# Masked queries shared between VectorE and ScalarE, and steps of short chains spread over their half-slots

## The chip, the cores and the metric

The kernel runs on one NeuronCore of a Trainium2 chip. A core has five engines that run side by side, each with a queue of its own, and wait for each other by semaphores: TensorE (PE in the profile; its weight loads are PEld), VectorE (DVE), ScalarE (ACT), GpSimd (POOL) and SyncE (SP, which here only issues DMAs). TensorE writes its results to PSUM, from which VectorE or ScalarE move them to SBUF. The metric is the device time of one execution in microseconds.

## What is computed

A decoder layer over 32 sequences of 128 tokens with 128 features, 16 heads of 8 features each: causal self-attention, cross-attention to a second input, and a mixture of 8 experts of which each token takes two. After each of the three comes a residual and a layer norm.

```python
def _attn(q_in, k_in, v_in, wq, bq, wk, bk, wv, bv, wo, bo, causal):
    Q = (q_in @ wq + bq).reshape(Bq, Sq, H, HD)
    Kp = (k_in @ wk + bk).reshape(Bq, Sk, H, HD)
    V = (v_in @ wv + bv).reshape(Bq, Sk, H, HD)
    scores = jnp.einsum('bqhd,bkhd->bhqk', Q, Kp) / jnp.sqrt(jnp.float32(HD))
    if causal:
        scores = jnp.where(mask, scores, -jnp.inf)
    a = jax.nn.softmax(scores, axis=-1)
    o = jnp.einsum('bhqk,bkhd->bqhd', a, V).reshape(Bq, Sq, Dm)
    return o @ wo + bo
...
x = _layernorm(x + _attn(x, x, x, ..., True), ln1_g, ln1_b)
x = _layernorm(x + _attn(x, encoder_output, encoder_output, ..., False), ln2_g, ln2_b)
x = _layernorm(x + _moe(x, router_w, router_b, e_w1, e_b1, e_w2, e_b2), ln3_g, ln3_b)
```

All arithmetic that matters here is in float32.

## The kernel before

**Stages.** First attention, then the experts. The attention works on groups of four sequences: eight groups of self-attention (named s0 to s7) and eight of cross-attention (c0 to c7). A unit is one sequence of one group, so there are 64 units, and units of s and c groups are interleaved in the list `order` (L1014). The experts' part runs 78 blocks of 128 rows, each with weights fetched from DRAM; its first blocks run beside the last steps of attention.

**Half-slots.** The attention is a software pipeline written out by hand. Each unit has two half-slots (`half_slot`, L1164). In half-slot h, TensorE first computes scores (`both_scores`, L437): for the unit t = h // 2 with queries as rows, eight heads at a time, into the PSUM buffer `sc` of which there is one, and for the unit t − 2 the same scores with keys as rows into `st`, of which there is one as well. VectorE takes the row maxima of `sc` (L487), which frees it; ScalarE takes the exponential of `st` (L495), which frees that. The maxima are split into three bfloat16 parts on GpSimd (`split`), turned round on TensorE and spread (`maxima`, L524, VectorE), and subtracted within the matmuls of `st`. In even half-slots TensorE also multiplies the probabilities of unit t − 3 with the values (`values`, 32 matmuls, evacuated by ScalarE at L541), in odd ones it turns the result round (`outputs`, two transposes, divided on VectorE at L552 and L553). Self-attention units have more matmuls for the causal mask (L442), and GpSimd clears the masked probabilities (L499).

**Masks of heads.** Heads lie four to a quarter of 32 partitions. A matmul that reads a quarter sees four heads at once, so the queries are stored four times, each time with all but every fourth head set to zero. `queries` (L400) projects two sequences at a time into a PSUM tile `pq` and writes the four masked copies into `qb` with four activations (L407) of 128 x 256, each as (pq + bias) times a mask column. A group has two such steps, so there are 32 of them and 128 activations. `qb` has four buffers; the experts' part uses the same ones later for `gt`.

**Steps beside the units.** Everything else of a group is cut into steps that are put into half-slots behind the work of the units: `turn_input` (transposes, evacuated by ScalarE), `keys`, `queries`, `values_of`, and after the group's units `turn_output` (two steps: transposes, evacuated by ScalarE at L564), `project` (seven steps: two projections with residual on VectorE at L573 and L576, then `normalize` at L331 with statistics on VectorE, the reciprocal root on GpSimd, and the scaling on ScalarE in two steps), then `hand_over` or `keep_x2` (four steps: two transposes with affine evacuation, two GpSimd steps). Cross-attention groups go on with `route`, `place`, `biases` and the scatter of their rows. `half_slot` calls the steps of its number from `table` in the order in which they were put there, and this is the order in the queues of all engines.

**The planner.** `chain(lo, hi, *parts)` (L1054) puts a list of steps, in order, into the half-slots lo to hi. Each step goes by `book` (L1043) to the half-slot in its window in which the busiest engine is least loaded; `busy` holds the loads, in microseconds estimated by hand, as a tuple of TensorE, VectorE, ScalarE and GpSimd. The costs of steps are given by `pe(us, act, dve)`, `dve` and `pool`. When a chain has more steps than half-slots are left, `book` gets an empty window and the steps at its front share the half-slot lo, until the remaining ones fit one to each.

For example the output chain of cross-attention group 0 has 13 steps for half-slots 45 to 54. Before, `turn_output` twice and both projections stand in 45, and the rest one to each half-slot from 46, with the last normalization step at 50 and `keep_x2` from 51. That of self-attention group 0 has five half-slots, 15 to 19, and its first nine steps (both `turn_output`, all seven of `project`) stand in 15.

**Fetches.** Groups 2 to 7 of self-attention are fetched by `fetch` (L118) on SyncE's queue, put at half-slot h0 − 15, where h0 is the first of the group's units. `xg` has three buffers, and one comes free when the group three before has added its residual in `project`. The same queue carries the packing of expert weights into DRAM, `pack` (two DMAs of 256 KB for each of the eight experts, at half-slots 4, 8, ... 32).

Of the kernel before, what the change touches and what calls it, by code (L numbers as in the profile page):

```python
# [8 lines left out]
F32 = mybir.dt.float32  # L9
# [4 lines left out]
AF = mybir.ActivationFunctionType  # L14
ALU = mybir.AluOpType
AX = mybir.AxisListType

P = 128
# [5 lines left out]
G = 4  # L24
# [38 lines left out]
def kernel(  # L63
# [34 lines left out]
    nc = tc.nc  # L98
# [6 lines left out]
    act = ctx.enter_context(tc.tile_pool(name="act", bufs=2))  # L105
# [74 lines left out]
    hmask = const.tile([P, 4], F32, name="hmask")  # L180
# [179 lines left out]
    def rowsof(g):  # L360
        return slice(32 * g, 32 * g + 32)
# [37 lines left out]

    def queries(gr):  # L400

        gr.qb = act.tile([P, G, 4, P], F32, tag="qb", name=f"qb_{gr.name}", bufs=4)
        for ab in PAIRS:
            pq = pair(f"pq_{gr.name}", ab)
            nc.tensor.matmul(pq, lhsT=gr.w.wq, rhs=gr.qT[:, ab], start=True, stop=True)
            for r in range(4):
                nc.scalar.activation(  # L407
                    gr.qb[:, ab, r, :], pq, AF.Identity,
                    bias=gr.w.bqm[:, r : r + 1], scale=hmask[:, r : r + 1],
                )  # L410
            yield

    turn = {"v": -1, "m": 0}
# [23 lines left out]
    def both_scores(new, old, half):  # L437


        def mask(g, i, j):  # L440
            k = slice(32 * j, P)
            nc.tensor.matmul(  # L442
                sc[:, i, :, k], lhsT=quarter[rowsof(g), j, :],
                rhs=bc(causal[rowsof(g), j, k], 1, 4), start=j == 0, stop=False,
            )

        def by_query(g, i, r):
            nc.tensor.matmul(  # L448
                sc[:, i, r, :], lhsT=new.group.qb[rowsof(g), new.b, r, :],
                rhs=new.group.k[rowsof(g), new.b, :],  # L450
                start=not new.masked, stop=not new.masked or r == 3,
            )

        def less_maxima(g, i, _):
            nc.tensor.matmul(
                st[:, i], lhsT=ones16[rowsof(g), :], rhs=old.mq[rowsof(g)], start=True, stop=False
            )

        def by_key(g, i, r):
            nc.tensor.matmul(  # L460
                st[:, i, r, :], lhsT=old.group.k[rowsof(g), old.b, :],
                rhs=old.group.qb[rowsof(g), old.b, r, :], start=False, stop=r == 3,
            )

        steps = []
        if new is not None:
            sc = ps_sc.tile([P, 2, 4, P], F32, tag="sc", name=f"sc_{new.name}_{half}")
            at_us = 0.0
            if new.masked:
                for j in range(RG):  # L470
                    steps.append((at_us, 1, mask, j))
                    at_us += 0.053 * (RG - j)
            for r in range(4):
                steps.append((at_us, 1, by_query, r))
                at_us += 0.222
        if old is not None:
            st = ps_st.tile([P, 2, 4, P], F32, tag="st", name=f"st_{old.name}_{half}")
            steps.append((0.0, 0, less_maxima, 0))
            steps += [(0.213 + 0.222 * r, 0, by_key, r) for r in range(4)]

        for _, query, do, n in sorted(steps, key=lambda step: step[:2]):
            for i in range(2):
                do(2 * (half if query else 1 - half) + i, i, n)
        if new is not None:
            if half == 0:
                new.m = small.tile([P, H], F32, tag="m", name=f"m_{new.name}")
            nc.vector.tensor_reduce(  # L487
                new.m[:, 8 * half : 8 * half + 8], sc.rearrange("p i r k -> p (i r) k"),
                AX.X, ALU.max,
            )  # L490
        if old is not None:
            if half == 0:
                old.pr = prob.tile([P, H, P], F32, tag="pr", name=f"pr_{old.name}")
            hs = slice(8 * (1 - half), 8 * (1 - half) + 8)
            nc.scalar.activation(  # L495
                old.pr[:, hs, :], st.rearrange("p i r k -> p (i r) k"), AF.Exp, scale=SCALE
            )
# [526 lines left out]
    def at(h, *call):  # L1024
        table.setdefault(h, []).append(call)
        return h + 1
# [3 lines left out]
    for t, u in enumerate(units):  # L1030
        for h, cost in (
# [8 lines left out]
            old = busy.get(2 * t + h, (0.0,) * 4)  # L1040
# [13 lines left out]
    def chain(lo, hi, *parts):  # L1054


        todo = []
        for made, *costs in parts:
            if len(costs) == 1:
                todo.append((costs[0], (made,)))  # L1060
                continue
            steps = []

            def step(made=made, steps=steps):
                if not steps:
                    steps.append(made())
                next(steps[0], None)

            todo += [(cost, (step,)) for cost in costs]
        ends = []  # L1070
        for n, (cost, call) in enumerate(todo):
            left = len(todo) - 1 - n
            end = book(lo, hi - left, cost, *call)
            lo = end if hi - end + 1 >= left else end - 1
            ends.append(end)
        return ends

# [9 lines left out]
    NORM = (dve(1.2), (0.0, 0.9, 0.0, 1.3), dve(0.2), dve(0.0, 0.7), dve(0.0, 0.7))  # L1087
    TURN = (pe(0.45, 0.4),) * 2
    PROJECT = (pe(0.45, 0.0, 0.4),) * 2
    ROUTE = (pe(0.3, 0.0, 0.9), dve(0.0, 0.2), dve(1.2), dve(1.1), dve(0.8), dve(0.4))  # L1090
    PLACE = (pe(0.2, 0.0, 1.0), pe(0.3, 0.0, 0.8), dve(1.6), dve(0.8), dve(0.6))
    behind = 2 * (len(units) + 2)
    sent = 0
    for gi in range(NG):
        s, c = groups["s", gi], groups["c", gi]
        h0, h3 = 2 * where["s", G * gi], 2 * where["s", G * gi + G - 1]
        h1, h2 = 2 * where["c", G * gi], 2 * where["c", G * gi + G - 1]
        if gi > 1:
            at(h0 - 15, fetch, s)
        chain(  # L1100
            max(h0 - 13, 1) if gi else -13, h0 - 2,
            (lambda s=s: turn_input(s), *TURN),
            (lambda s=s: keys(s), *TURN),
            (lambda s=s: queries(s), pe(0.45, 1.6), pe(0.45, 1.6)),
        )
        chain(max(h0 - 1, 0) if gi else -2, h0 + 4, (lambda s=s: values_of(s), *TURN))
        book(max(h0 + 1, 7), h3 + 8, pool(1.3), residual, s)
        ends = chain(
            h3 + 9, min(h3 + 24, h1 - 5),
            (lambda s=s: turn_output(s), *TURN),  # L1110
            (lambda s=s: project(s), *PROJECT, *NORM),
            (lambda s=s, c=c: hand_over(s, c), *TURN, pool(1.3), pool(1.3)),
        )
        at(h1 - 18, fetch, c)
        chain(
            h1 - 14, h1 - 7,
            (lambda c=c: turn_input(c), *TURN),
            (lambda c=c: keys(c), *TURN),
        )
        chain(  # L1120
            max(h1 - 9, ends[10]), h1 - 2,
            (lambda c=c: queries(c), pe(0.45, 1.6), pe(0.45, 1.6)),
        )
        chain(h1 - 1, h1 + 4, (lambda c=c: values_of(c), *TURN))
        ends = chain(
            h2 + 9, h2 + 18,
            (lambda c=c: turn_output(c), *TURN),
            (lambda c=c: project(c), *PROJECT, *NORM),
            (lambda c=c: keep_x2(c), *TURN, pool(1.3), pool(1.4)),
        )  # L1130
        ends = chain(ends[10], ends[10] + 5, (lambda c=c: route(c), *ROUTE))
        ph = phases[next(p for p, (g0, n) in enumerate(PHASES) if gi < g0 + n)]
        ends = chain(ends[-1], ends[-1] + 4, (lambda c=c, ph=ph: place(c, ph), *PLACE))
        h = ends[3]
        chain(h, h + 5, (lambda c=c: biases(c), dve(0.6), pe(0.1, 0.3), pe(0.45, 0.0, 0.6), pool(0.0)))
        h = max(h, sent)
        for b in range(G):
            for k in range(2):
                at(h, scatter, c, ph, b, k)
                h += 1  # L1140
        sent = h
        if gi == PHASES[0][1] - 1:
            ready = h
# [137 lines left out]
```

## Time and profile before

| what | us |
|---|---|
| median of three runs | 656.05 (651.39 to 667.48) |
| the profiled execution | 655.68 |
| its span | 654.0 |
| maxima of `sc` (L487, VectorE), 128 | 156.4 |
| exponentials of `st` (L495, ScalarE), 128 | 131.7 |
| masked queries (L407, ScalarE), 128 | 61.9 |
| evacuations of the output transposes (L564, ScalarE), 32 | 11.0 |

The page gives for each engine its busy time and share of the span, the span in 40 slices with the busy tenths of each, the clock granted to TensorE in each slice (9 is nearly full speed, 5 is half), and groups of instructions with their mean duration. A matmul's busy time is modelled, so a busy TensorE isn't one at its peak. The masks of L407 show a mean of 0.576 us, but four in a row take 1.93 us, since one starts before the other has fully ended.

### The profile page before, as it was taken

Reading aid. Unit: us, or ns where it says so; the run is one execution under the profiler, and the core shown is the slowest. Engines: PE = TensorE matmul, PEld = TensorE weight load, DVE = VectorE, ACT = ScalarE, POOL = GpSimd, SP = SyncE. Lnnn points to the kernel's source line nnn. Section 1 sums busy time; section 2 is a strip of 40 time slices with the busy share of each in tenths; the row PEclk is TensorE's granted clock in tenths of the full one; section 3 lists DMA queues with packets and bytes.
Section 4 is the critical chain, followed back from the end, with each engine's and each line's share of the span. In section 5 each row is a group of like instructions: output and inputs, shape, how many; then the busy total and the mean of one; then the engine's idle time right before and its main releaser. Section 6 shows DMA issues by size and latency. Waiting matters only on the chain. (4 is left out here: it accounts for less than half of the span.)

```text
span 654.0 us, 22743 instructions
## 1 busy us (share of the span) xinstructions
PE 583.4 (89%) x9247; PEld 497.4 (76%) x9247; DVE 410.7 (63%) x1327; ACT 404.4 (62%) x919; POOL 368.6 (56%) x749
## 2 busy tenths in 40 slices
PE   8999899999998999999999988988897978999870
PEld 7777787878876777777876866777797878998870
DVE  3345456665667766786787778884867634543563
ACT  4266576787677468667758676645674446665652
POOL 3256465544645557538737525633788885664561
PEclk9599899999999899999999999987999979999995
DMA  6110610832010011001001100422897989999972
GB/s 130 35 35 4 122 43 3 244 136 66 4 34 3 11 47 32 3 7 56 10 20 34 35 4 14 167 71 73 264 285 261 351 306 365 375 344 383 349 254 70
DMA packets 48041, 82.53 MB, mean 126 GB/s; under 512 B 7968, under 2 KB 26464, under 8 KB 47936
## 3 DMA queue, kind: packets, MB, share of 16 engines
q1 hardware_dynamic: 42816, 71.57, 34.3%
q0 software_dynamic: 4544, 9.38, 3.9%
q8 instruction: 72, 1.18, 0.7%
q14 instruction: 33, 0.27, 0.1%
q10 hardware_dynamic: 576, 0.13, 0.1%
HBM read 62.15 MB, written 23.10 MB: 130 GB/s over the span
## 5 line engine op out<-in xcount | busy, mean ns | idle before, releaser
L893 ACT ACTIVATE h<-ph,wd 128x128 f32<-128x128 f32 x312 | 88.7, 369 | 63.3 <-PE ph L888 21.3
L487 DVE TENSOR_REDUCE m_s<-sc_s 128x8 f32<-128x1024 f32 x64 | 78.3, 1223 | 76.6 <-PE sc_s L448 75.6
L499 POOL TENSOR_SCALAR_AFFINE_SELECT pr_s<-pr_s 128x1024 f32<-128x1024 f32 x64 | 69.9, 1092 | 84.4 <-ACT pr_s L495 84.1
L911 POOL DMA_INDIRECT eo<-ot,to x78 | 77.8, 997 | 55.2 <-DVE acc L996 13.5
L495 ACT ACTIVATE pr_c<-st_c 128x1024 f32<-128x1024 f32 x64 | 65.9, 1029 | 60.7 <-PE st_c L460 60.7
L487 DVE TENSOR_REDUCE m_c<-sc_c 128x8 f32<-128x1024 f32 x64 | 78.1, 1220 | 31.0 <-PE sc_c L448 19.5
L888 PE MATMUL ph<-xT,wd 128*128 128x128 f32 x624 | 86.7, 284 | 9.9 <-DMA wd<-wpk 5.2
L495 ACT ACTIVATE pr_s<-st_s 128x1024 f32<-128x1024 f32 x64 | 65.8, 1028 | 42.9 <-PE st_s L460 42.2
L888 PEld LDWEIGHTS ph<-xT,wd 128*128 128x128 f32 x624 | 78.3, 197 | 14.7 <-DMA wd<-wpk 4.1
L904 PE MATMUL po<-wd,h 128*128 128x128 f32 x624 | 84.6, 280 | 4.9 <-ACT h L893 4.9
L904 PEld LDWEIGHTS po<-wd,h 128*128 128x128 f32 x624 | 77.9, 195 | 5.5 <-ACT h L893 5.5
L448 PE MATMUL sc_c<-k_c,qb_c 32*128 32x128 f32 x1024 | 75.5, 286 | 6.7 <-DVE m_c L487 5.1
L448 PE MATMUL sc_s<-k_s,qb_s 32*128 32x128 f32 x1024 | 76.2, 289 | 0.0
L448 PEld LDWEIGHTS sc_c<-k_c,qb_c 32*128 32x128 f32 x1024 | 63.2, 189 | 12.4 <-DVE m_c L487 7.8
L460 PE MATMUL st_c<-qb_c,k_c 32*128 32x128 f32 x1024 | 71.7, 279 | 0.0
L784 POOL DMA_INDIRECT xs<-x,slots x64 | 64.3, 1005 | 12.8 <-issue 12.2
L460 PE MATMUL st_s<-qb_s,k_s 32*128 32x128 f32 x1024 | 71.6, 278 | 0.0
L460 PEld LDWEIGHTS st_s<-qb_s,k_s 32*128 32x128 f32 x1024 | 67.0, 190 | 0.9
L460 PEld LDWEIGHTS st_c<-qb_c,k_c 32*128 32x128 f32 x1024 | 67.3, 191 | 0.2
L448 PEld LDWEIGHTS sc_s<-k_s,qb_s 32*128 32x128 f32 x1024 | 66.9, 198 | 0.3 <-issue 0.2
L909 DVE COPY ot<-po 128x128 f32<-128x128 f32 x78 | 22.5, 290 | 63.8 <-PE po L904 56.7
L442 PE MATMUL sc_s<-causal,quarter 32*128 32x512 bf16 (+3 forms) x512 | 48.4, 309 | 4.2 <-DVE m_s L487 4.0
(247 smaller groups left out, 1202.8 us busy)
## 6 DMA issues: line engine op xcount, KB each, us to landing
wd<-wpk SPq DMA_DIRECT2D x78, 514.0 KB, 5.4
xs<-blank SPq DMA_DIRECT2D x2, 2600.0 KB
xt<-xs SPq DMA_DIRECT2D x20, 260.0 KB, 6.0
wpk<-in_L_xattn_e_w_dram SPq DMA_DIRECT2D x16, 256.0 KB, 9.5
gt<-eo SPq DMA_DIRECT2D x8, 512.0 KB, 7.0
xg<-in_x_dram SPq DMA_DIRECT2D x8, 256.0 KB, 4.8
eg<-in_ctx_dram SPq DMA_DIRECT2D x8, 256.0 KB
x2d<-base SPq DMA_DIRECT2D x8, 256.0 KB
```

The lines of the kernel that those rows point to most:

```text
L442: nc.tensor.matmul(sc[:, i, :, k], lhsT=quarter[rowsof(g), j, :], rhs=bc(causal[rowsof(g), j, k], 1, 4), start=j == 0, stop=False,)
L448: nc.tensor.matmul(sc[:, i, r, :], lhsT=new.group.qb[rowsof(g), new.b, r, :], rhs=new.group.k[rowsof(g), new.b, :], start=not new.masked, ...
L460: nc.tensor.matmul(st[:, i, r, :], lhsT=old.group.k[rowsof(g), old.b, :], rhs=old.group.qb[rowsof(g), old.b, r, :], start=False, stop=r == 3,)
L487: nc.vector.tensor_reduce(new.m[:, 8 * half : 8 * half + 8], sc.rearrange("p i r k -> p (i r) k"), AX.X, ALU.max,)
L495: nc.scalar.activation(old.pr[:, hs, :], st.rearrange("p i r k -> p (i r) k"), AF.Exp, scale=SCALE)
L499: nc.gpsimd.affine_select(out=old.pr[:, hs, :], in_=old.pr[:, hs, :], pattern=[[0, 8], [1, P]], compare_op=ALU.is_ge, fill=0.0, base=0, ch ...
L784: i = nc.gpsimd.indirect_dma_start(out=xs[ph.p][:, :], out_offset=bass.IndirectOffsetOnAxis(ap=slots[:, k, t : t + 1], axis=0), in_=gr.x2[ ...
L888: nc.tensor.matmul(hid[:, c, :], lhsT=w[:, c * P : (c + 1) * P], rhs=self.xT[i // XB][:, i % XB, :], start=True, stop=True,)
L893: nc.scalar.activation(self.h[i][:, c, :], hid[:, c, :], AF.Gelu, bias=w[:, B1 + c : B1 + c + 1])
L904: nc.tensor.matmul(po, lhsT=h[:, c, :], rhs=w[:, W2 + c * P : W2 + (c + 1) * P], start=c == 0, stop=c == NFC - 1,)
L909: nc.vector.tensor_copy(ot, po)
L911: s = nc.gpsimd.indirect_dma_start(out=eo[p][:, :], out_offset=bass.IndirectOffsetOnAxis(ap=self.to[q][:, i % XB : i % XB + 1], axis=0), i ...
```

## The change

It has three parts.

1. `queries`: the first two masked copies stay on ScalarE, one activation each. The other two are made by one VectorE instruction over 128 x 512 elements: (pq + bias) times mask, where pq is read twice and the two mask columns are spread along it. So that each engine writes a simple piece, `qb` changes its order from (sequence, mask, query) to (mask, sequence, query), and the matmuls that read it follow. The booked cost of a step goes from 0.45 on TensorE and 1.6 on ScalarE to 0.45, 0.96 on ScalarE and 0.65 on VectorE (`ASK`).
2. `chain`: if a chain has more steps than half-slots, its steps are spread evenly, step n of N into half-slot lo + n × (half-slots) // N. The output chain of cross-attention group 0 becomes: both `turn_output` in 45, projections in 46 and 47, statistics and aggregation both in 48, the rest of the normalization in 49, 50 and 51, `keep_x2` from 51. That of self-attention group 0: `turn_output` and the first projection in 15, the second projection and the statistics and aggregation in 16, then two steps in 17 and the last in 18, both transposes of `hand_over` in 18.
3. The fetch of a self-attention group is put no earlier than the half-slot behind the second projection of the group three before it (`free`), and its chain two half-slots later at the earliest. Fetches of groups 3, 4 and 6 go from half-slots 11, 25 and 53 to 17, 29 and 54.

With the other costs, the planner books some further steps in other half-slots of their windows.

```diff
     def queries(gr):
 
-        gr.qb = act.tile([P, G, 4, P], F32, tag="qb", name=f"qb_{gr.name}", bufs=4)
+        gr.qb = act.tile([P, 4, G, P], F32, tag="qb", name=f"qb_{gr.name}", bufs=4)
         for ab in PAIRS:
             pq = pair(f"pq_{gr.name}", ab)
             nc.tensor.matmul(pq, lhsT=gr.w.wq, rhs=gr.qT[:, ab], start=True, stop=True)
-            for r in range(4):
+            for r in range(2):
                 nc.scalar.activation(
-                    gr.qb[:, ab, r, :], pq, AF.Identity,
+                    gr.qb[:, r, ab, :], pq, AF.Identity,
                     bias=gr.w.bqm[:, r : r + 1], scale=hmask[:, r : r + 1],
                 )
+            nc.vector.scalar_tensor_tensor(
+                gr.qb[:, 2:4, ab, :].rearrange("p r b q -> p r (b q)"),
+                bc(pq.rearrange("p b q -> p (b q)"), 1, 2), gr.w.bq, bc(hmask[:, 2:4], 2, 2 * P),
+                ALU.add, ALU.mult,
+            )
             yield
...
         ends = []
+        if len(todo) > hi - lo + 1:
+            for n, (cost, call) in enumerate(todo):
+                h = lo + n * (hi - lo + 1) // len(todo)
+                ends.append(book(h, h, cost, *call))
+            return ends
         for n, (cost, call) in enumerate(todo):
...
+    ASK = (pe(0.45, 0.96, 0.65),) * 2
...
+    free = {}
...
         if gi > 1:
-            at(h0 - 15, fetch, s)
+            at(max(h0 - 15, free.get(gi - 3, 0)), fetch, s)
         chain(
-            max(h0 - 13, 1) if gi else -13, h0 - 2,
+            max(h0 - 13, 1, free.get(gi - 3, 0) + 2) if gi else -13, h0 - 2,
...
-            (lambda s=s: queries(s), pe(0.45, 1.6), pe(0.45, 1.6)),
+            (lambda s=s: queries(s), *ASK),
...
+        free[gi] = ends[3]
...
-            (lambda c=c: queries(c), pe(0.45, 1.6), pe(0.45, 1.6)),
+            (lambda c=c: queries(c), *ASK),
```

More of the change, by code (lines that the diff above doesn't have):

```diff
@@ L448, in by_query @@
             nc.tensor.matmul(
-                sc[:, i, r, :], lhsT=new.group.qb[rowsof(g), new.b, r, :],
+                sc[:, i, r, :], lhsT=new.group.qb[rowsof(g), r, new.b, :],
                 rhs=new.group.k[rowsof(g), new.b, :],
@@ L461, in by_key @@
                 st[:, i, r, :], lhsT=old.group.k[rowsof(g), old.b, :],
-                rhs=old.group.qb[rowsof(g), old.b, r, :], start=False, stop=r == 3,
+                rhs=old.group.qb[rowsof(g), r, old.b, :], start=False, stop=r == 3,
             )
```

## The prediction

> **What bounds the kernel now.** I read the page first (busy shares and slices), then the waits of TensorE, then ten-microsecond windows over the attention stage, and last the timeline around each idle stretch.
>
> ```profile
> span 654.0 us, 22743 instructions
> PE 583.4 (89%) x9247; PEld 497.4 (76%) x9247; DVE 410.7 (63%) x1327; ACT 404.4 (62%) x919; POOL 368.6 (56%) x749
> ...
> PEclk9599899999999899999999999987999979999995
> ```
>
> TensorE (PE) is busy 89% of the span. The attention stage runs from about 30 to 440 us (the row maxima at L487 run from 12.6 to 428.1 us, 128 of them, so a half-slot is about 3.2 us). Summed from the windows, PE is idle about 27 us there. After 440 us come the expert blocks, with the DMA share near 1.0; the chain of waits starts at 530 us and lies wholly in them. The change does not touch them, so a microsecond won in attention brings them, and the end, forward by one.
>
> So the question is what becomes of those 27 us. The waits of TensorE name most of them:
>
> ```profile
> PE sc_c L448 <- DVE m_c L487: 5.1, 6, 1.7
> ...
> PE py_c L573 <- ACT oT_c L564: 4.6, 7, 2.0
> PE sc_s L442 <- DVE m_s L487: 4.0, 6, 1.6
> PE st_c L455 <- ACT pr_c L495: 3.3, 6, 0.9
> PE st_s L455 <- ACT pr_s L495: 3.1, 4, 1.3
> ...
> PE st_c L455 <- ACT pr_s L495: 1.1, 2, 0.5
> ```
>
> Columns: total us, times, longest. Three kinds: VectorE (DVE) late with the maxima that free the single score buffer, ScalarE (ACT) late with the exponential that frees the other one, and a projection that waits for its own evacuation just ahead of it.
>
> One case of the second kind, ScalarE in the timeline and then TensorE:
>
> ```profile
> 319.24 1.93 ACT L407 ACTIVATE qb_c<-pq_c,bqmc,hmask 128x256 f32<-128x256 f32 x4
> 321.05 1.03 ACT L495 ACTIVATE pr_s<-st_s 128x1024 f32<-128x1024 f32 x1
> 322.14 0.39 PE L455 MATMUL st_c<-mq_c,ones 32*128 32x512 bf16 x2 [0.53 <-ACT pr_s L495]
> ```
>
> Four masked queries hold ScalarE for 1.93 us, the exponential starts behind them, and PE stands 0.53 us. The last pieces are the clock in windows around the one bunched chain, at 70 us, and the prices:
>
> ```profile
> 70.00:80.00 10.00, 7.61 (x125) 6.44 (x117) 4.46 (x16) 5.02 (x10) 4.16 (x7) 0.83 0.89 170
> 210.00:220.00 10.00, 7.36 (x121) 5.98 (x120) 8.30 (x23) 3.91 (x7) 4.27 (x8) 0.83 0.01 2
> L407 ACT ACTIVATE qb_c<-pq_c,bqmc,hmask 128x256 f32<-128x256 f32 x64 | 31.0, 576 | 2.4 <-PE pq_c L405 2.4
> L996 DVE SCALAR_TENSOR_TENSOR acc<-gt,wts,acc 128x128 f32<-128x128 f32 x64 | 18.0, 344 | 2.6 <-DMA gt<-eo 2.5
> L626 DVE TENSOR_TENSOR base<-pb,x 128x512 f32<-128x512 f32 x8 | 5.5, 685 | 2.2 <-PE pb L624 2.2
> ```
>
> The third column from the right is the granted clock. 0.83 over 10 us is 1.7 us of TensorE time lost, on top of the idle time itself.
>
> **The change, part by part.**
>
> *Queries on ScalarE.* 128 activations become 64. Their mean is 0.576 us, but four in a row take 1.93, so 0.45 each behind the first; a step falls from 1.93 to 0.565 + 0.45 = 1.02, and 32 steps free 29 us. What PE gets of it are the gaps behind a query step: six of them (at 104.4, 143.6, 146.6, 262.3, 322.1 and 352.9 us) of 0.69, 0.74, 0.53, 0.56, 0.53, 0.93, together **4.0**. All are shorter than or about the 0.9 us by which the exponential comes earlier, so I take all away. [...]
>
> *The instruction added on VectorE.* 32 of 128x512 out of PSUM. No row has that form. The nearest, L626, has the same size, its source in PSUM and one SBUF tensor: 0.685. Scaling L996 (344 ns for 128 elements) by the slope between L553 (291 ns, 128) and L626 gives 344 + 394 = 0.74. I take 0.69; 32 make 22 us, on an engine busy two thirds of the attention stage and 96% between 340 and 350 us.
>
> *Its wait.* In the built order of the changed kernel, all 32 of these instructions wait for ScalarE, not for TensorE: the two halves of a step run one after the other. The trace of before has no PSUM tile read by two engines, so nothing there prices it. [...] Worked on the case above: projection done at 319.21, two activations to 320.26, the VectorE instruction from about 320.35 to 321.04; the next maxima, which started at 320.86, stand behind it in VectorE's queue and start 0.2 late. Where the units are unmasked the scores are done some 0.35 us sooner, so 0.55 late. If both halves could run at once it would be done at 319.95 and cost nothing. Behind the maxima waits the next use of the score buffer on PE; in even half-slots the 1.08 us of values covers it, in odd ones nearly nothing, and 15 of the 32 steps are in even half-slots, so that their delay falls into odd ones. Lateness 32 x 0.3 = 9.6, half of it passed on: **4.8**. Bounds: 0 (all covered) and 32 x 0.69 = 22 (none covered); below nothing is excluded, since the instruction only adds work to VectorE and its relief on ScalarE is counted above.
>
> *Chains spread.* The rule bites where a chain has more steps than half-slots: the eight output chains of cross-attention (13 steps in 10), those of the first and the last self-attention group, and the input chain of group 1. Before, both output transposes and both projections of a cross-attention group stood in one half-slot, so the projection had to wait for ScalarE's copy; now the projections are one and two half-slots on. That removes L573's **4.6** and 0.4 of its self-attention twin. In the first group nine steps stood in half-slot 15; the gaps there are 0.99 (transposes waiting for the normalized rows) and 1.34 (exponential behind four normalizations), plus 1.7 of clock: 4.0. It is spread over four half-slots, but its second hand-over still shares one with the normalization it reads, so I leave 0.5: **3.5**.
>
> What is late next: statistics and aggregation of each cross-attention group (4 x 0.277 and 4 x 0.15 on VectorE, about 1.2 us in a row) now share a half-slot. With 1.22 of maxima and 0.42 of mask product that is 2.9, under 3.2, so covered; where routing or placing is in the same half-slot (68, 114, 122) VectorE has 3.8 to 4.1 us and the cover is gone: up to 3.9. Against that, 0.84 us of residual additions leaves the half-slots 83, 99, 119 and 127, where VectorE was over: about 2.9 back. Net **+1**.
>
> *Fetches and queues.* The fetches of self-attention groups 3 and 4 go from half-slots 11 and 25 to 17 and 29, that of 6 from 53 to 54. On SyncE's queue two weight packings now stand ahead of the fetch of group 3 instead of behind it, and one ahead of group 4's. Before, that fetch waited in the queue for its buffer until 70.1 us anyway and held the packings. The first transposes come two or three half-slots (6 to 9 us) after the buffer is free, a fetch lands in 4.8: covered; if that cover fails, 2 us each. The packings start earlier, where the DMA share is 0.01 to 0.13: nothing. The new costs of a query step also let the planner book some steps elsewhere (by one to six half-slots, the queries of cross-attention group 5 from 101 and 102 to 95 and 98): the same instructions within the windows they had, nothing. GpSimd's instructions are the same ones, the reciprocal roots one half-slot later and one residual addition eight: nothing, since their users move along.
>
> *Sum.* −4.0 − 5.0 − 3.5 + 4.8 + 1 = −6.7. The profiled execution took 655.7 with its launch (span 654.0), beside a median of 656.05: **649**.
>
> **Rivals.**
>
> *More is won (640).* VectorE's delays are covered (0 for 4.8), and the two half-speed stretches at 211 and 220 us, 1.7 each, which follow 1.6 us gaps behind placing, do not come again: 655.7 − 12.5 + 1 − 3.4 = 641. For it: VectorE waited 75.6 us for the masked scores, so it has room in the first half. Against: between 280 and 440 us VectorE is already at 0.8 to 0.96 in many windows, and twelve query steps fall there.
>
> *VectorE becomes the bound (671, slower).* One mechanism: the added instruction sits at the head of VectorE's queue, waiting for ScalarE, and every maximum behind it is late by its whole length. Price 32 x 0.69 = 22, and each gap over about 1.6 us brings half speed, say four times 1.7 = 7: 655.7 − 12.5 + 1 + 22 + 7 = 673; I carry 671. It turns slower by 2% (13 us) when a step costs PE about 0.75 us in the mean, that is when ScalarE is itself behind an exponential when it gets the projection. Half-slot 37 with two query steps shows the place.
>
> *The change does little (656).* The steps do move, but the gaps return elsewhere: the 4.6 and 3.5 come back as late maxima. This lies inside the likeliest case's outer range.
>
> **Numbers.** Likeliest, 649, own range 643 to 656 with the rival "little": 0.53. More is won: 0.30. VectorE bound: 0.17. The span of the three runs before is 2.4% of their median, so 2% (13.1 us, below 642.9 or above 669.2) is about what a measurement can tell from no change. Faster 0.31 (the second case and a sliver of the first), slower 0.16, within 0.53. The range 637 to 665 leaves out the far ends of the two rivals.
>
> **What would show it.** Right: no wait of py_c for oT_c over 1 us in total; the waits of st for pr behind a query step gone; the new instruction near 0.69, starting right behind ScalarE's second activation; first clock dip at 70 us gone. Wrong: waits of sc for the maxima grow from 10.5 us by more than 10, or the new instruction lasts over 0.8.

## The result, and the profile after

| kernel | median, us | lowest to highest | runs |
|---|---|---|---|
| before | 655.96 | 651.39 to 667.48 | 10 |
| changed | 651.27 | 647.00 to 661.45 | 10 |

The ratio is 0.9933 with a 95% interval of 0.9903 to 0.9962: 4.4 us won, within 2%. A second comparison, in which the kernel before took 657.66, gave 655.50 and a ratio of 0.9985 (0.9944 to 1.0026). So the change is worth between nothing and one per cent. The profile of the first comparison fell on an execution of 657.72, the second highest of its ten; the lines below are of the second profile (652.50, span 650.6). The idle stretches of TensorE that are named for this kernel have the same lengths in both to 0.02 us, except one of 0.55 (0.3 in the first); the clock behind them does not, as is said further on.

The page of the changed kernel, busy times and granted clock:

```profile
span 650.6 us, 22713 instructions
...
PE 578.0 (89%) x9247; PEld 491.8 (76%) x9247; DVE 433.9 (67%) x1359; ACT 378.9 (58%) x855; POOL 368.1 (57%) x749
...
PEclk9599899999999899999999998997999889999995
```

VectorE has 23.2 us more and ScalarE 25.5 less than before (410.7 and 404.4); the prediction had 22 and 29, and the masks on ScalarE alone went from 61.9 to 32.5. The bound is unchanged: TensorE at 89%. What it waits for, changed kernel (us in total, times, longest):

```profile
PE sc_c L453 <- DVE m_c L492: 9.2, 11, 2.2
PE sc_s L447 <- DVE m_s L492: 9.0, 8, 2.9
...
PE st_c L460 <- ACT pr_c L500: 3.9, 7, 1.4
...
PE sc_c L453 <- DVE m_s L492: 1.7, 4, 1.1
...
PE st_c L460 <- ACT pr_s L500: 0.8, 2, 0.5
PE st_s L460 <- ACT pr_c L500: 0.6, 2, 0.3
...
PE sc_s L447 <- DVE m_c L492: 0.3, 1, 0.3
```

Three things are to be seen. The wait of the cross-attention projection (4.6 before) has no row left. The waits for the exponential fell from 7.5 to 5.3 only. And the waits for the maxima doubled, from 10.5 to 20.2. Together, with the 0.4 and 0.2 of self-attention's own projections, the three kinds stood at 23.0 before and stand at 25.7 now: the gaps did not go away, they changed hands.

The new instruction, and what is left on ScalarE (busy time, mean ns, idle time before them):

```profile
L407 ACT ACTIVATE qb_c<-pq_c,bqmc,hmask 128x256 f32<-128x256 f32 x32 | 16.3, 560 | 1.6 <-PE pq_c L405 1.2
L411 DVE SCALAR_TENSOR_TENSOR qb_c<-pq_c,bqc,hmask 128x512 f32<-128x512 f32 x16 | 12.0, 750 | 9.0 <-ACT qb_c L407 8.8
L411 DVE SCALAR_TENSOR_TENSOR qb_s<-pq_s,bqs,hmask 128x512 f32<-128x512 f32 x16 | 11.9, 748 | 9.1 <-ACT qb_s L407 9.1
```

It takes 0.75 us, and VectorE stands 17.9 us in all waiting for ScalarE's two masks ahead of it. The query step that the prediction worked through, now in the timeline of the changed kernel (start, duration, idle time before it and its releaser):

```profile
317.74 1.02 ACT L407 ACTIVATE qb_c<-pq_c,bqmc,hmask 128x256 f32<-128x256 f32 x2
318.96 1.02 ACT L500 ACTIVATE pr_s<-st_s 128x1024 f32<-128x1024 f32 x1 [0.20 <-PE st_s L465]
...
318.80 0.75 DVE L411 SCALAR_TENSOR_TENSOR qb_c<-pq_c,bqc,hmask 128x512 f32<-128x512 f32 x1 [1.12 <-ACT qb_c L407]
319.46 1.21 DVE L492 TENSOR_REDUCE m_s<-sc_s 128x8 f32<-128x1024 f32 x1
...
320.73 0.38 PE L453 MATMUL sc_c<-k_c,qb_c 32*128 32x128 f32 x2 [0.30 <-DVE m_s L492]
```

The step went almost as foretold. Two masks last 1.02; the exponential now waits for its scores (0.20) and no longer for the masks. VectorE idles 1.12, works 0.75, and the maxima start behind it. The gap of 0.53 behind the exponential became one of 0.30 behind the maxima.

**Where the first chain's gain went.** The two gaps at 73 and 75 us are gone, and a single longer one stands in their place. The timeline of the changed kernel there, VectorE, GpSimd and TensorE:

```profile
71.70 0.36 DVE L340 BATCH_NORM_AGGREGATE mv_s<-st_s 128x2 f32<-128x6 f32 x4
73.97 1.18 DVE L246 CAST d_at<-d_at_i 128x248 f32<-128x248 int32 x1 [1.91 <-POOL d_at_i L244]
75.08 1.21 DVE L492 TENSOR_REDUCE m_s<-sc_s 128x8 f32<-128x1024 f32 x1
...
72.48 1.05 POOL L342 TENSOR_TENSOR rs_s<-rs_s,mhalf 128x4 f32<-128x4 f32 x1
73.50 0.44 POOL L244 IOTA d_at_i<- 128x248 int32 x1
...
76.34 0.39 PE L447 MATMUL sc_s<-causal,quarter 32*128 32x512 bf16 x2 [2.62 <-DVE m_s L492]
```

Half-slot 16 holds a one-time piece of set-up: GpSimd counts out a constant `d_at` (L293, through `counted`, L242 to L246) and VectorE casts it to float. Spread, the normalization of group s0 put its aggregation and its root into this half-slot too, and they come first. GpSimd gets to the count-out only behind the root, VectorE's cast stands 1.91 us for it, takes 1.18, and the maxima of the next half-slot, which free the score buffer, are queued behind the cast. Before, the whole normalization stood in half-slot 15. VectorE waited for the count-out even longer then, but nothing was late for it: the next maxima had to wait for their scores anyway, which TensorE, behind its two gaps, delivered 1.28 us after VectorE was free. The kernel before, VectorE:

```profile
76.96 0.29 DVE L246 CAST d_at<-d_at_i 128x248 f32<-128x248 int32 x1 [2.73 <-POOL d_at_i L244]
78.53 1.22 DVE L487 TENSOR_REDUCE m_s<-sc_s 128x8 f32<-128x1024 f32 x1 [1.28 <-PE sc_s L448]
```

Windows of the changed kernel at the two places (length; busy us of PE, PEld, DVE, ACT, POOL; granted clock, DMA share, GB/s):

```profile
70.00:80.00 10.00, 7.38 (x125) 6.32 (x128) 6.07 (x17) 3.81 (x7) 4.93 (x10) 0.85 0.76 164
...
210.00:220.00 10.00, 5.74 (x119) 4.58 (x120) 9.21 (x23) 3.33 (x6) 4.56 (x8) 1.00 0.01 2
220.00:230.00 10.00, 9.84 (x162) 8.27 (x161) 6.71 (x20) 5.67 (x10) 4.25 (x9) 0.83 0.05 15
```

So the dip of the clock at 70 us (0.83 before) stayed as well, at 0.85. In the first profile of the changed kernel it is deeper: 0.94, and 0.55 in the ten microseconds behind.

**Two places farther on.** At placing (220 us) the gap behind the maxima grew from 1.62 to 2.88, and where the first expert block waits for its input, from 1.69 to 3.28. (The 1.62 is not a fixed part of the kernel before: a second profile of it, below, has no gap there.)

```profile
220.16 0.39 PE L447 MATMUL sc_s<-causal,quarter 32*128 32x512 bf16 x2 [2.88 <-DVE m_s L492]
...
443.85 2.08 PE L893 MATMUL ph<-xT,wd 128*128 128x128 f32 x8 [3.28 <-DVE xT L885]
```

In the second, residual, statistics and aggregation of cross-attention group 6 stand with routing in VectorE's queue ahead of the copy L885; before, part of them stood elsewhere.

### The profile page after: what moved, and what is told of

It reads as the page before. It is cut to its first block, busy times and chain, and to the rows that moved or that the text cites. A ratio compares the mean times of both kernels' runs of the same rounds, so it can differ in the third digit from the quotient of the medians.

```text
span 655.9 us, 22713 instructions
## 1 busy us (share of the span) xinstructions
PE 583.9 (89%) x9247; PEld 496.1 (76%) x9247; DVE 434.5 (66%) x1359; ACT 379.8 (58%) x855; POOL 368.8 (56%) x749
## 3 DMA queue, kind: packets, MB, share of 16 engines
q8 instruction: 72, 1.18, 0.8%
## 4 chain that ended last, share of the span: by engine, by line
PE 62%; DVE 20%; DMA 8%; ACT 4%; issue 3%; POOL 3%; SPq 0%; ACTq 0%; DVEq 0%; POOLq 0%
PE ph L893 8%; PE po L909 7%; PE sc_s L453 6%; PE sc_c L453 6%; PE po_s L539 4%; DMA wd<-wpk 4%; DVE m_c L492 4%; PE st_s L465 4%; PE po_c L539 4%; PE sc_s L447 3%; DVE m_s L492 3%; DMA eo<-ot,to 2%; PE st_s L460 2%; PE st_c L460 2%; PE pk_s L396 1%
## 5 line engine op out<-in xcount | busy, mean ns | idle before, releaser
L504 POOL TENSOR_SCALAR_AFFINE_SELECT pr_s<-pr_s 128x1024 f32<-128x1024 f32 x64 | 70.1, 1096 | 82.6 <-ACT pr_s L500 82.2
L465 PEld LDWEIGHTS st_c<-qb_c,k_c 32*128 32x128 f32 x1024 | 65.9, 188 | 0.2
```

The lines of the kernel that those rows point to most:

```text
L465: nc.tensor.matmul(st[:, i, r, :], lhsT=old.group.k[rowsof(g), old.b, :], rhs=old.group.qb[rowsof(g), r, old.b, :], start=False, stop=r == 3,)
L504: nc.gpsimd.affine_select(out=old.pr[:, hs, :], in_=old.pr[:, hs, :], pattern=[[0, 8], [1, P]], compare_op=ALU.is_ge, fill=0.0, base=0, ch ...
```

## The experiments

My theory after the result: the spreading is worth its 7.5 us, and the queries give them back through VectorE's wait at the head of its queue. The rival: the spreading itself runs into something new (the count-out is the candidate), and the wait matters little.

**The two halves of the change, apart.** First the queries and later fetches with the old rule for chains:

```diff
-        if len(todo) > hi - lo + 1:
-            for n, (cost, call) in enumerate(todo):
-                h = lo + n * (hi - lo + 1) // len(todo)
-                ends.append(book(h, h, cost, *call))
-            return ends
```

> The queries split between the two engines (and the later fetches, which its costs need), but the old rule for short chains. My theory: ScalarE's relief wins 4.0 us and VectorE's late maxima take 4.8 or, with the measured 0.75 us of the new instruction, a little more: ratio to the kernel before 0.998 to 1.006; the waits of the projection for its own evacuation (4.6 us) and the 70 us gap are back. Rival, the gain of the whole change comes from the queries: ratio 0.991 to 0.995.

Then the spreading and later fetches, with all four masks on ScalarE at the old costs and in the old layout of `qb`:

```diff
-    ASK = (pe(0.45, 0.96, 0.65),) * 2
+    ASK = (pe(0.45, 1.6),) * 2
...
-            for r in range(2):
+            for r in range(4):
...
-            nc.vector.scalar_tensor_tensor(
...
```

> The chains spread and the fetches later, but all four masks on ScalarE with the old costs. My theory: 5.0 and 3.5 us won, 1 lost to late maxima: ratio 0.985 to 0.992, better than the whole change; the waits of TensorE for the maxima stay within 3 us of the 10.5 before. Rival, the spreading only moves the gaps: ratio 0.997 to 1.003, and the waits for the maxima grow by 5 us or more though VectorE has no added work.

On this chip the kernel before took 677.72. Queries alone: 678.65, ratio 1.0008 (0.9968 to 1.0047). Spread alone: 676.88, ratio 0.9986 (0.9951 to 1.0021). The first agrees with what the prediction's terms give (−4.0 and +4.8), within an interval of some 5 us. The second does not: −7.5 us was expected of it, and one is there. TensorE's waits of the kernel with the spreading alone:

```profile
PE sc_s L442 <- DVE m_s L487: 9.0, 7, 3.1
...
PE sc_c L448 <- DVE m_c L487: 5.7, 6, 2.2
PE st_c L455 <- ACT pr_c L495: 5.0, 9, 1.2
...
PE sc_c L448 <- DVE m_s L487: 2.0, 4, 1.0
```

16.7 us for the maxima, 6.2 more than before, with no work added to VectorE. The gap of 2.63 at 76.32 us is there, and one of 3.10 at placing. With the queries alone neither the gap at 76 nor the 3.3 at the first expert block appears, and the projection waits again (2.6 for the copy and 1.0 for routing ahead of it). So the spreading does remove the projection's wait, and loses it again to gaps at 76 us and ahead of the experts that are its own making: the rival. The gap at placing is not: it stands with the queries alone as well, at 2.88.

**The order of the two engines.** VectorE first, then ScalarE's two masks:

```diff
+            nc.vector.scalar_tensor_tensor(
+                gr.qb[:, 2:4, ab, :].rearrange("p r b q -> p r (b q)"),
...
             for r in range(2):
                 nc.scalar.activation(
...
-            nc.vector.scalar_tensor_tensor(
...
```

> The whole change, but in each query step VectorE's instruction comes first and ScalarE's two activations wait for it. My theory (the wait at the head of VectorE's queue is what costs): VectorE's wait for ScalarE, 19.5 us, disappears, TensorE's waits for the maxima fall by 3 to 6 us from 19.8; ScalarE ends a step some 0.85 us later than in the change, so that TensorE's waits for the exponential rise by 2 to 4 us from 5.3; ratio 0.990 to 0.996. Rival (VectorE's 24 us of added work is what costs, not the wait): the waits for the maxima stay near 20 us, ratio 0.993 to 1.000.

687.26, ratio 1.0118 (1.0071 to 1.0165), so slower by about 1.2%. (The 19.5 and 19.8 of the expectations are of the first profile.) ScalarE's waits and then TensorE's in this kernel:

```profile
ACT qb_c L412 <- DVE qb_c L406: 20.8, 15, 2.6
ACT qb_s L412 <- DVE qb_s L406: 19.8, 14, 3.6
...
PE st_c L460 <- ACT pr_c L500: 8.5, 11, 2.4
PE sc_s L447 <- DVE m_s L492: 6.6, 5, 2.6
PE sc_c L453 <- DVE m_c L492: 5.4, 5, 2.2
```

The waits for the maxima fell to 13.1 as I expected, but the ones for the exponential rose to 16.5: it is now ScalarE that stands 40.6 us behind a busy VectorE, twice what VectorE stood before, and the exponentials queue there. My number (0.990 to 0.996) was wrong: I had priced only the wait I removed.

**No order at all.** Each sequence of a pair in a PSUM tile of its own; ScalarE makes the four masks of one, VectorE those of the other:

```diff
+            pa = mm_tile([P, P], f"pqa_{gr.name}_{ab.start}")
+            pv = mm_tile([P, P], f"pqv_{gr.name}_{ab.start}")
...
+                nc.scalar.activation(
+                    gr.qb[:, r, a, :], pa, AF.Identity,
...
+            nc.vector.scalar_tensor_tensor(
+                gr.qb[:, :, v, :], bc(pv, 1, 4), gr.w.bq, bc(hmask, 2, P), ALU.add, ALU.mult,
+            )
```

> The whole change, but a query step projects its two sequences into two PSUM tiles; ScalarE makes the four copies of one, VectorE in one instruction the four of the other, so neither waits for the other. My theory: the waits for the maxima fall by 3 to 6 us from 19.8, those for the exponential stay within 2 us of 5.3 (ScalarE's step is about 0.2 us longer), ratio 0.982 to 0.989. Rival (added work, not the wait): as the change, 0.991 to 0.996; a second PSUM tile per step may add waits of the small matmuls for their buffers.

681.66, ratio 1.0053 (1.0016 to 1.0089). VectorE no longer waits for ScalarE, and the waits for the maxima are 13.0, but ScalarE's pieces of 128 elements cost 0.46 each, hardly less than the 0.56 of 256, so ScalarE has 48.1 us of masks instead of 32.5; the waits for the exponential are 7.9. My 0.982 to 0.989 was wrong too. The first expert block starts at 452.6 us, against 451.9 with the spreading alone on the same chip. Why the fewer waits bring no time in this kernel I did not find.

**The same kernels again.** The kernel before and the changed one, on the chip of the next kernels:

> The kernel before once more, for a profile from the same chip as the next three: every theory expects a ratio of 1.00, TensorE's waits for the maxima near 10.5 us and the projection's wait for its evacuation near 4.6.

> The change once more, on the chip of its neighbours: if the two parts are worth what they measured by themselves (1.0008 and 0.9986), 0.997 to 1.002; if the first result holds on every chip, 0.990 to 0.996. TensorE's longest wait for the maxima, 2.6 us near 76 to 79 us, is there again in either case.

655.50 for the changed kernel, ratio 0.9985 (0.9944 to 1.0026), and 657.84 for the kernel before, in one execution. This has the same waits as the first profile of that kernel, but for the maxima: 8.9 us instead of 10.5, since the gap of 1.62 at placing is not there. The last instruction of placing ahead of these maxima, kernel before, first and second profile:

```profile
218.41 1.05 DVE L756 TENSOR_TENSOR slots<-si,ri 128x8 uint32<-128x8 uint32 x1
...
219.46 0.17 DVE L756 TENSOR_TENSOR slots<-si,ri 128x8 uint32<-128x8 uint32 x1
```

So this gap comes and goes between executions of one kernel.

**VectorE's wait taken away.** Its instruction is issued one half-slot later, behind the maxima of that half-slot, when ScalarE is long done:

```diff
+            deferred.append((gr, pq, ab))
...
+    def other_masks():
+        while deferred:
+            gr, pq, ab = deferred.pop(0)
+            nc.vector.scalar_tensor_tensor(
...
         both_scores(unit(t), unit(t - 2), half)
+        other_masks()
```

> The whole change, but VectorE's instruction of a query step is put into the next half-slot, behind the maxima of that half-slot. My theory (the instruction costs because it waits for ScalarE ahead of the maxima): VectorE's wait for ScalarE falls from 19.5 us to under 5, TensorE's waits for the maxima by 3 to 5 us, ratio to the change 0.991 to 0.996. Rival (its 24 us on VectorE cost, wherever they stand): waits for the maxima as in the change, ratio to the change 0.998 to 1.003.

657.76, ratio 1.0028 (0.9990 to 1.0066). The instruction's row, and TensorE's waits:

```profile
L419 DVE SCALAR_TENSOR_TENSOR qb_c<-pq_c,bqc,hmask 128x512 f32<-128x512 f32 x16 | 11.9, 742 | 0.0
...
PE sc_s L454 <- DVE m_s L499: 9.8, 9, 2.9
PE sc_c L460 <- DVE m_c L499: 8.9, 11, 2.2
```

VectorE's idle time ahead of it is 0.0, and the maxima are as late as in the changed kernel (9.0 and 9.2). So taking the standstill away by doing the work later wins nothing. Nor are the 0.75 us of work the cause by themselves: in the two kernels in which VectorE does the same work early the maxima wait 13.1 and 13.0, and with the spreading alone, without this work, they wait 13.6 when the gap of 3.10 at placing is left out. What counts, by these runs, is when in the half-slot the work is done, and done early it is ScalarE's queue that pays (whose waits can also cover some for the maxima).

**The count-out, one step sooner.** It is issued on GpSimd with the step of set-up before it, in half-slot 14; the cast stays where it was:

```diff
         nc.vector.tensor_tensor(lower, e_row, e_col, ALU.is_lt)
+        i = setup.tile([P, max(ND), E], I32, name="d_at_i")
+        nc.gpsimd.iota(i, pattern=[[1, max(ND)], [0, E]], base=NS, channel_multiplier=0)
         yield
-        later["d_at"] = counted([P, max(ND), E], [[1, max(ND)], [0, E]], NS, "d_at")
+        later["d_at"] = const.tile([P, max(ND), E], F32, name="d_at")
+        nc.vector.tensor_copy(later["d_at"], i)
```

> The whole change, but the GpSimd instruction that counts out the routing constant d_at is issued one step sooner, in half-slot 14, so that VectorE does not stand in half-slot 16 waiting for it behind the reciprocal root of the first group. Theory (this wait ate what spreading the first chain had won): the 2.6 us gap near 77 us falls under 1, and the half speed behind it goes; ratio to the change 0.990 to 0.996. Rival (the maxima are late there by the added steps alone): the gap stays over 2 us, ratio to the change 0.998 to 1.002.

> The kernel with the early count-out once more, as the base for the next two and because its first interval was wide: 0.985 to 0.993 against the kernel before if that gain is real; 0.996 to 1.001 if it was chance.

649.83, ratio 0.9892 (0.9831 to 0.9953), against 0.9985 for the changed kernel in the same comparison; in a later one 648.65, ratio 0.9929 (0.9891 to 0.9967). The same stretch of VectorE's timeline and the window, kernel with the early count-out:

```profile
71.68 0.36 DVE L343 BATCH_NORM_AGGREGATE mv_s<-st_s 128x2 f32<-128x6 f32 x4
71.96 0.25 DVE L296 CAST d_at<-d_at_i 128x248 f32<-128x248 int32 x1
72.17 1.23 DVE L495 TENSOR_REDUCE m_s<-sc_s 128x8 f32<-128x1024 f32 x1
...
70.00:80.00 10.00, 8.71 (x177) 7.20 (x175) 6.26 (x19) 6.09 (x13) 5.18 (x10) 1.00 0.77 164
```

The cast takes 0.25 and waits for nothing, the maxima come 2.9 us sooner (1.9 of it the wait, 0.9 the cast itself, which took 1.18 in the changed kernel, where GpSimd's L504 ran beside it from 73.91 to 75.02), the gap of 2.62 is gone (one of 1.24 ahead of the next transposes remains), and the clock stays at 1.00. The edit touches nothing else, so the cause of this gap is shown. For the clock it is less sure: it is 1.00 there in all five profiles with the edit, but also in that of the queries alone, with the gaps of before, and in that with a tile for each engine, with the gap of 2.62.

The gap at placing went with it, which I had not aimed at. It goes with where GpSimd's work falls. In the changed kernel, three instructions of placing on VectorE, and GpSimd's beside them:

```profile
215.62 0.88 DVE L755 CAST si<-sf 128x8 uint32<-128x8 f32 x1
...
216.80 0.93 DVE L759 TENSOR_TENSOR ri<-ri 128x8 uint32<-128x8 uint32 x1
...
217.85 1.12 DVE L761 TENSOR_TENSOR slots<-si,ri 128x8 uint32<-128x8 uint32 x1
...
215.12 1.35 POOL L598 TENSOR_TENSOR x<-y_s,lng 128x512 f32<-128x512 f32 x1
216.60 1.12 POOL L504 TENSOR_SCALAR_AFFINE_SELECT pr_s<-pr_s 128x1024 f32<-128x1024 f32 x1
217.69 1.25 POOL L600 TENSOR_TENSOR x<-x,lnb1c 128x512 f32<-128x512 f32 x1
```

Each of the three ends within 0.03 us of a GpSimd instruction's end (216.50 and 216.47, 217.73 and 217.72, 218.97 and 218.94). With the early count-out the cast takes 0.86 and again ends with a GpSimd instruction (213.54 and 213.52), but the two others fall into a pause of GpSimd, from there to 214.93, and take 0.17 each: 1.7 us of VectorE ahead of the maxima. In the first profile of the kernel before, L756 took 1.05 and ended at 219.46, a GpSimd instruction beside it at 219.44; in the second it took 0.17. So these 1.7 us go with the phase between the two engines. Why the three last longer beside GpSimd's work, no run here shows.

**The spreading with the early count-out, four masks on ScalarE.** The kernel of the spreading alone with the edit just shown:

> The chains spread, the count-out early, all four masks on ScalarE. Theory (the spreading is worth what the prediction gave it once the wait for GpSimd is out of its way; the queries bring about nothing): 0.985 to 0.992, equal to the version with the queries within 0.004. Rival (the two parts need each other: without ScalarE's relief the spreading brings nothing): 0.995 to 1.001.

644.89, ratio 0.9874 (0.9825 to 0.9923), against 0.9986 without the edit (on another chip, each to the kernel before there). That is 8.3 us, the interval from 5.1 to 11.5: the 7.5 of the theory is in it, though the gap at placing, absent here, may have part in it. Page and TensorE's waits of this kernel:

```profile
PE 573.7 (90%) x9247; PEld 489.7 (76%) x9247; DVE 412.4 (64%) x1327; ACT 404.2 (63%) x919; POOL 368.2 (57%) x749
...
PE sc_c L451 <- DVE m_c L490: 6.1, 7, 2.2
...
PE st_c L458 <- ACT pr_c L498: 3.7, 7, 1.2
PE sc_s L445 <- DVE m_s L490: 3.2, 5, 1.0
...
PE st_s L458 <- ACT pr_s L498: 1.7, 3, 0.7
```

It has the lowest time and ratio of all the kernels here, below both comparisons of the changed one (0.9933 and 0.9985, the first with an interval that just overlaps), and it has none of the masks on VectorE. Beside the kernel with both (0.9929 on the same chip): the maxima wait 10.2 instead of 14.5, the exponentials 6.5 instead of 5.3, the first expert block starts at 433.9 instead of 439.3. So moving two masks costs 4.3 on one side and brings 1.2 on the other. The runs of the two kernels, from one comparison, hardly touch: six from 642.42 to 645.73, and twelve with the masks from 645.45 to 653.44, medians 3.8 us apart. So beside the spreading and the early count-out, the masks on VectorE cost time, which the waits had said. With the chains as before they cost nothing that could be measured (1.0008 for the queries alone).

**Two smaller suspects**, both on the kernel with masks and early count-out. First, the projections share a half-slot, and statistics and aggregation have one each:

```diff
                 h = lo + n * (hi - lo + 1) // len(todo)
+                if hi - lo == 9:
+                    h = lo + (0, 0, 1, 1, 2, 3, 4, 5, 6, 6, 7, 8, 9)[n]
```

> The early count-out, and in the output chains of cross-attention both projections share a half-slot and statistics and aggregation get one each. Theory (the shared half-slots make VectorE late): the 3.3 us wait for the first transposed rows of the experts' part falls to under 2, waits of TensorE for the maxima fall by 1 to 3 us from 15; ratio to its base 0.994 to 0.998. Rival (covered, as the prediction mostly had it): within 0.002 of its base.

648.86, ratio 0.9920 (0.9879 to 0.9960), beside 0.9929: no difference. The wait ahead of the first expert block did fall, from 3.28 to 2.27, but a projection waits 1.15 for routing, and the gap of 2.88 at placing is back, which its base does not have. So the equality holds as a total; what the shared half-slot alone costs stays open between nothing and about what that gap costs, 2.9 us and whatever clock goes with it.

Second, the tables of placing are filled in half-slots 40 and 42, ahead of their use:

```diff
-            nc.gpsimd.memset(ph.fill, float(-P))
...
+    def tables(p):
...
+        at(40 + 2 * p, tables, p)
```

> The early count-out, and the four small placing tables of each phase are filled by GpSimd in half-slots 40 and 42 instead of at their first use. The same theory at another place (VectorE stands at the head of its queue for a GpSimd instruction that is behind others): VectorE's 1.5 us wait for the table at 204 us and the 2.0 us gap of TensorE at 207 us shrink by 1 us or more, the 0.6 us gap near 378 us goes; ratio to its base 0.994 to 0.998. [...]

647.83, ratio 0.9914 (0.9870 to 0.9957). The gap of 2.03 that stood at 208.27 us in its base is gone, and the one of 2.88 at placing is back, at 214.08: taken away here, returned a few us on, and the total can't be told from its base. The gap near 378 us, which I had expected to go, is there at 0.57.

## Why the prediction came out so

The total (649, found 651.27, and 655.50 in the second comparison) and "within 2%" were right, but in good part by luck. The prediction put its 6.7 us into the attention, and they are not there: from the first maxima to the first expert block it is 432.6 and 432.0 us in the two profiles of the kernel before, 433.9 and 431.9 in those of the changed one (425.2 and 427.5 with the early count-out, 421.5 with the spreading and the early count-out alone). What the profiles show shorter is the rest, which the prediction said was not touched: 208.8 and 209.9 before, 207.6 and 206.8 changed. Why, no run here shows. Term by term, two were off in size or cause, and one failed.

- **Fetches and queues, at nothing: right.** The only wait of a transposition for a fetch is the one of 0.6 at the start, at 4.4 us, before any moved fetch.
- **Projections, −5.0: right.** 4.6 became less than 0.3, and came back in part (3.6) with the old rule.
- **ScalarE's relief, −4.0: right mechanism, too large.** A step fell to 1.02 as worked out. The waits for the exponential fell by 2.2, not 4.0. The gaps at 143.6 and 146.6 went wholly; others came anew (0.54 at 308.7, where a normalization and the copy L588 stand beside the masks; 1.45 at 378.4, where the exponential stands behind two scalings of a normalization; it is there with the spreading alone too, at 1.23, where the projection's longest wait, 2.03, had stood, so it belongs to that term). I had summed the gaps behind query steps and not asked what else reaches ScalarE once the phases shift.
- **VectorE's instruction, +4.8: right size, reason not borne out.** It lasts 0.75, not 0.69: the scaled estimate of 0.74 was the better of the two, since it came from rows of the same operation. The cost on the maxima is 4.3, by the kernels with and without it. But with the wait for ScalarE that I put at its root taken away, by doing the work one half-slot later, the maxima are as late as ever (19.3, after 20.2). Done early, the same work makes them no later, and ScalarE's exponentials late instead. So it is a matter of when the work is done; the wait alone does not explain it.
- **The first group's chain, −3.5: failed.** The step that failed is "it is spread over four half-slots", with a remainder of 0.5 for the hand-over. The remainder of the gaps is 1.24 (the kernel with the early count-out; 2.33 before), with the clock whole, so 2.8 of the 4.0 could be had. But for GpSimd the prediction said "the reciprocal roots one half-slot later: nothing, since their users move along". The root's users do, yet the count-out in that half-slot came to stand behind it, the cast behind that, and the maxima behind the cast: 2.62 and 0.55 of gaps, and a clock of 0.85, where 0.99, 1.34 and 0.83 had been. That line was wrong, and it cost the whole term and 0.8 more.
- **Statistics and aggregation in one half-slot, +1: about right in size, at another place.** I named half-slots with routing or placing (68, 114, 122). The gap that can be tied to it is ahead of the experts, 1.6 more, where routing and the hand-over to the experts meet it.
- **Not in the sum:** the gap at placing, 1.26 more with a shift against GpSimd. It is there with either part alone (3.10 and 2.88), and against the second profile of the kernel before, which has none, it is 2.88 more: a matter of phase, not of the change's parts.

Added up as measured: −2.2 − 4.8 + 0.8 + 4.3 + 1.6 + 1.3 = +1.0, where the 0.8 is 3.17 of gaps and 1.7 of clock at the first chain now, against 2.33 and 1.7, each from one profile. That agrees with the length of the attention, which did not get shorter. The two comparisons say −4.4 and −1.0 for the whole kernel, each uncertain by 2 to 3 us; the difference lies outside these waits and is not resolved.

Of the rivals, "VectorE becomes the bound" did not come: the maxima wait 9.7 us more, where it needed 22. Its price for the clock, half speed behind each gap over about 1.6 us, was my estimate from two stretches of the first profile of the kernel before (211 and 220 us), and no run shows it as a rule: in that same profile the clock is 1.00 behind the gap of 2.03 us near 379 us (see the last section). "The change does little", with the gaps returning as late maxima, is what came, and I had given it too small a place, inside the likeliest case. My own mark for wrong, over 10 us more on the maxima, was all but reached (9.7), and is passed when the second profile of the kernel before is the base (11.3).

## What to carry to other kernels

When a step is put into another half-slot, go through every queue that it touches and ask what stands behind each of its instructions there, up to the one that frees the buffer that the bound engine waits for; a piece of set-up with a wait in it, harmless where it was, is easily the next one behind. Try the parts of a change apart and on one chip: here a part that could gain and a part that could not looked like one small gain, and the first alone, with a small repair, gained more by its median (8.3 us) than the whole did in either comparison (4.4 and 1.0). Profile the same kernel twice: a gap that comes and goes between two executions must not be charged to a change. And an engine with a good share of idle time (VectorE at 63%) is not free: it idles in half-slots where nothing is late, and the added work stands in those where something is.

## What the runs showed of the hardware

- **The chips here differed more than most of the changes.** The median of the kernel before was 655.96 to 657.66 in three comparisons and 677.72 on another chip. Most of that lies in the experts' part: from the first expert block to the end it is 206.8 to 209.9 us in the four profiles of the kernel before and the changed one, and on that chip 224.4 (queries alone) and 222.9 (spreading alone). So only ratios within one comparison are set beside each other here.
- **The same gap costs the clock in one execution and not in another.** The gap of 2.03 us ahead of a projection near 379 us is in both profiles of the kernel before: from 377 to 382 us the clock is 1.00 in the first, 0.66 in the second, which is 1.7 us. Behind the gap of 2.62 at the first chain it lost nothing in one kernel (a tile for each engine), 1.7 us in the second profile of the changed kernel and 5.1 in its first. So 1.7 us of clock cannot be booked for every gap over 1.6. What makes the difference, no run here shows.
- **The added instruction has a steady price.** A mean of 0.74 to 0.75 us in the changed kernel and in the three that move it (VectorE first, by sequence, VectorE later), while the small operation L761 of placing takes from 0.17 to 1.98 in the changed kernel.
